# Layer 1's cross-attention in a two-layer decoder: scores on row halves, mask by a product, values stationary on column quarters

## The chip, the cores and the metric

The kernel is one program on one core of a Trainium2 chip. TensorE (PE) multiplies into PSUM; VectorE (DVE), ScalarE (ACT) and GpSimd (POOL) work on the results; SyncE (SP) issues most transfers. The metric is the device time of one execution in microseconds, the median of the runs shown.

## What is computed

Two decoder layers on x of 2 x 1024 x 256, f32. Each layer is attention, cross-attention to a context of 64 tokens, and a feed-forward part, each followed by a residual sum and a layer norm. The change concerns layer 1's cross-attention:

```python
qh = (q @ wq.T).reshape(bs, sq, N_HEADS, D_K).transpose(0, 2, 1, 3)      # 16 heads of 16
kh = (k @ wk.T).reshape(bs, sk, N_HEADS, D_K).transpose(0, 2, 1, 3)      # k = v = ctx_1024, 64 tokens
vh = (v @ wv.T).reshape(bs, sk, N_HEADS, D_K).transpose(0, 2, 1, 3)
z = jnp.einsum('bhqd,bhkd->bhqk', qh, kh) / math.sqrt(D_K)
z = jnp.where(mask[:, None, :, :], jnp.float32(-10000000000.0), z)
z = jax.nn.softmax(z, axis=-1)
z = jnp.einsum('bhqk,bhkd->bhqd', z, vh)
return z.transpose(0, 2, 1, 3).reshape(bs, sq, D_MODEL) @ wo.T
x = _layernorm(x + ...)
```

## The kernel before

The parts run one after the other: `l0_attn`, `l0_xattn`, `l0_ffn` (eight experts, 32 steps of one expert and one group of 512 rows), `l1_attn`, `l1_xattn`, `l1_ffn`. A group is 512 rows (NG = 4), a tile 128 rows (NT = 16), four tiles to a group.

`prepare` makes what layer 1 needs (transposed weights, `lxkT`, `vblk`, the mask, the quantised feed-forward weights). It is a generator: from step 4 of `l0_ffn` on, each step asks it for one piece (up to its next `yield`), and after the last step the rest is taken. Before the change it has 24 pieces, and 29 steps ask.

`l1_xattn` first spreads the keys: `kblk` (line 1644, VectorE) holds for each batch the 64 keys of each head in that head's 16 rows and zero elsewhere, so that one product of 128 rows and 512 columns makes the scores of eight heads. Then, tile by tile:

- `queries(g)`: the queries of a group, transposed (line 1661), scaled on the way out of PSUM by ScalarE and VectorE.
- `softmax(n)`: GpSimd fills a tile `lxp` with -1e10 (line 1673), two products make the 1024 scores (line 1676), VectorE copies those that the mask keeps over the fill (line 1680), takes the maximum of each head (line 1685), GpSimd subtracts it (line 1686), ScalarE takes the exponential (line 1687).
- `turn(n)`: eight transposes (line 1697) and two copies, one by ScalarE and one by VectorE.
- `mix(n)`: eight products with the turned weights stationary and `vblk` moving, 34 columns each; every head's block has a column of ones, so that the sum of the exponentials comes out beside the values (line 1712). VectorE takes the reciprocal (line 1717) and multiplies (line 1719).
- `back(n)`: two transposes of the result (line 1729). `output(n)`: the product with wo (line 1743), the residual, and at the third and fourth tile of a group the layer norm and the maximum of |x| into `xm` (line 1756), which `l1_ffn` starts from.

The last group of `l1_attn` is still open here: `ends` are its four last steps (transposes at 1394, output product at 1409 added to r = x + bias, the norm, transposes of the result at 154).

Only TensorE's order is written out by hand in this part; the order on the other engines is the scheduler's:

```python
queries(0); softmax(0); softmax(1)
for n in range(NT + 3):
    if n < 4: self.ends[n]()
    if n % 4 == 1 and n // 4 + 1 < NG: queries(n // 4 + 1)
    softmax(n + 2)
    if n < NT: turn(n)
    output(n - 3); back(n - 2); mix(n - 1)
```

PSUM: `bank()` rotates over three buffers, `wide()` (scores) over two, `acc()` is one.

Of the kernel before, what the change touches and what calls it, by code (L numbers as in the profile page):

```python
# [18 lines left out]
P = 128  # L19
B, S, D = 2, 1024, 256  # L20
T = B * S
NG = 4
# [11 lines left out]
class Decoder:  # L34
# [11 lines left out]
    def pool(self, name, bufs, **kw):  # L46

        return self.tc.tile_pool(name=name, bufs=bufs, reuse_waits="tile", **kw)
# [1459 lines left out]
    def prepare(self, tmp):  # L1508
# [8 lines left out]
        self.keep = late.tile([P, T // P, SK], U8, name="keep")  # L1517
        nc.vector.tensor_scalar(self.keep, mask, 0.0, None, ALU.is_equal)
# [3 lines left out]
        )  # L1522
        yield
        wT = {}
# [42 lines left out]
        self.vblk = late.tile([P, B, 8, 2, 17], F32, name="vblk")  # L1567
        nc.gpsimd.memset(self.vblk, 0.0)
        for k in range(2):
            rows = slice(k * SK, (k + 1) * SK)  # L1570
            nc.gpsimd.memset(self.vblk[rows, :, :, k, 16:17], 1.0)
            for b in range(B):
                nc.vector.tensor_copy(
                    self.vblk[rows, b, :, k, 0:16],
                    ps[rows, b * D : (b + 1) * D].rearrange("p (m k i) -> p m k i", k=2, i=16)[:, :, k, :],
                )
# [60 lines left out]
    def l1_xattn(self):  # L1637
# [4 lines left out]
        for b in range(B):  # L1642
            for m in range(2):
                nc.vector.tensor_tensor(
                    kblk[:, b, m],
                    self.lxkT[:, m, b * SK : (b + 1) * SK].unsqueeze(1).to_broadcast(blk),
                    self.ofhead.unsqueeze(2).to_broadcast(blk), ALU.mult,
                )
        self.xm = self.late.tile([P, 2 * NG + 1], F32, name="xm")
        with ExitStack() as s:  # L1650
            pool = lambda n, k: s.enter_context(self.pool(n, k))
            qp, pp, ptp, op = pool("lxq", 2), pool("lxp", 4), pool("lxpT", 3), pool("lxo", 3)
            qT, prob, turned, tok, tokT, res, new = {}, {}, {}, {}, {}, {}, {}
            wide = [P, H, SK]

            def queries(g):
                qT[g] = qp.tile([P, 2, GT], F32, tag="lxqT", name="lxqT")
                for m in range(2):
                    ps = self.bank()
                    for c in range(2):  # L1660
                        nc.tensor.matmul(
                            ps, lhsT=self.lxwqT[:, c, m * P : (m + 1) * P], rhs=self.xT[g][:, c, :],
                            start=c == 0, stop=c == 1,
                        )
                    self.evac(qT[g][:, m, :], ps, 0.25)

            def softmax(n):

                if n >= NT:
                    return  # L1670
                g, i = divmod(n, 4)
                p = pp.tile(wide, F32, tag="lxp", name="lxp")
                nc.gpsimd.memset(p, -1e10)
                ps = self.wide()
                for m in range(2):
                    nc.tensor.matmul(
                        ps[:, m, :], lhsT=qT[g][:, m, i * P : (i + 1) * P],
                        rhs=kblk[:, g // 2, m].rearrange("p h k -> p (h k)"), start=True, stop=True,
                    )
                nc.vector.copy_predicated(  # L1680
                    p, self.keep[:, n, :].unsqueeze(1).to_broadcast(wide),
                    ps.rearrange("p m (h k) -> p (m h) k", k=SK),
                )
                nm = self.sm.tile([P, H], F32, tag="lxnm", name="lxnm")
                nc.vector.tensor_reduce(nm, p, AX.X, ALU.max, negate=True)
                nc.gpsimd.tensor_tensor(p, p, nm.unsqueeze(2).to_broadcast(wide), ALU.add)
                nc.scalar.activation(p, p, AF.Exp)
                prob[n] = p

            def turn(n):  # L1690
                p = prob.pop(n)
                turned[n] = ptp.tile([P, 8, P], F32, tag="lxpT", name="lxpT")
                for half in range(2):
                    ps = self.bank()
                    for k in range(4):
                        m = half * 4 + k
                        nc.tensor.transpose(
                            ps[:, k * P : (k + 1) * P],
                            p[:, 2 * m : 2 * m + 2, :].rearrange("p h k -> p (h k)"), self.ident,
                        )  # L1700
                    self.evac(
                        turned[n][:, half * 4 : half * 4 + 4, :], ps.rearrange("p (k q) -> p k q", q=P),
                        by=nc.vector if half else nc.scalar,
                    )

            def mix(n):

                if not 0 <= n < NT:
                    return
                ps = self.acc()[:, 0 : H * 17].rearrange("p (h i) -> p h i", i=17)  # L1710
                for m in range(8):
                    nc.tensor.matmul(
                        ps[:, 2 * m : 2 * m + 2, :], lhsT=turned[n][:, m, :],
                        rhs=self.vblk[:, n // 8, m].rearrange("p a i -> p (a i)"), start=True, stop=True,
                    )
                rz = self.sm.tile([P, H], F32, tag="lxrz", name="lxrz")
                nc.vector.reciprocal(rz, ps[:, :, 16])
                tok[n] = op.tile([P, D], F32, tag="lxtok", name="lxtok")
                nc.vector.tensor_tensor(
                    tok[n].rearrange("p (h i) -> p h i", i=16), ps[:, :, 0:16],  # L1720
                    rz.unsqueeze(2).to_broadcast([P, H, 16]), ALU.mult,
                )

            def back(n):
                if not 0 <= n < NT:
                    return
                ps = self.bank()
                for c in range(2):
                    nc.tensor.transpose(
                        ps[:, c * P : (c + 1) * P], tok[n][:, c * P : (c + 1) * P], self.ident  # L1730
                    )
                tokT[n] = op.tile([P, 2, P], F32, tag="lxtokT", name="lxtokT")
                self.evac(tokT[n].rearrange("p c q -> p (c q)"), ps[:, 0:D], by=nc.scalar)

            def output(n):
                if not 0 <= n < NT:
                    return
                g, i = divmod(n, 4)
                if i == 0:
                    res[g] = self.rp.tile([P, 4, D], F32, tag="r", name="r")  # L1740
                ps = self.bank()[:, 0:D]
                for c in range(2):
                    nc.tensor.matmul(
                        ps, lhsT=tokT[n][:, c, :], rhs=self.lxwoT[:, c, :], start=c == 0, stop=c == 1
                    )
                nc.vector.tensor_tensor(res[g][:, i, :], ps, self.x[g][:, i, :], ALU.add)
                if i == 1:
                    new[g] = self.xp.tile([P, 4, D], F32, tag="x", name="xg")
                tiles = {2: range(3), 3: range(3, 4)}
                if g == NG - 1:  # L1750
                    tiles = {1: range(2), 2: range(2, 3), 3: range(3, 4)}
                tiles = tiles.get(i)
                if tiles:
                    self.normalise(new[g], res[g], tiles)
                    k = 2 * g + i - (1 if g == NG - 1 else 2)
                    nc.vector.tensor_reduce(
                        self.xm[:, k : k + 1], new[g][:, tiles.start : tiles.stop, :], AX.XY, ALU.max,
                        apply_absolute_value=True,
                    )
                if i == 3:  # L1760
                    self.x[g] = new[g]

            with self.tc.manual_schedule(engines={mybir.EngineType.PE}):
                queries(0)
                softmax(0)
                softmax(1)
                for n in range(NT + 3):
                    if n < 4:
                        self.ends[n]()
                    if n % 4 == 1 and n // 4 + 1 < NG:  # L1770
                        queries(n // 4 + 1)
                    softmax(n + 2)
                    if n < NT:
                        turn(n)
                    output(n - 3)
                    back(n - 2)
                    mix(n - 1)
# [4 lines left out]
    def l1_ffn(self, out):  # L1782
# [4 lines left out]
        with ExitStack() as s:  # L1787
# [57 lines left out]
            nc.scalar.activation(early, self.xm[:, 2 * NG :], AF.Silu)  # L1845
# [258 lines left out]
```

## Time and profile before

| what | value |
|---|---|
| time, median of 3 runs | 2337.06 us (2333.24 to 2337.58) |
| the profiled execution | 2335.84 us |
| its span in the profile | 2333.8 us |
| busy in the span: PE, DVE, ACT, POOL | 2255.8, 1666.6, 1105.9, 906.3 us |
| `l1_xattn`, first query product to last maximum | 2133.94 to 2251.62 us |

The profile's page gives busy time by engine, the chain of work that ended last, and groups of instructions: line, engine, operation, output from input with shapes, count, then busy microseconds and mean nanoseconds of one, then the engine's idle time just before them and what ended most of it. A table of stretches gives the busy time of each engine in a stretch, with the TensorE clock that was granted (1.00 is full). An f32 matmul shows as two instructions in the trace. L70, L74 and L76 are the lines of the helper that copies out of PSUM.

### The profile page before, as it was taken

To read this page: it belongs to the slowest core of one execution; us is meant where nothing else is said; L and a number is where in the kernel's file an instruction comes from. 1 tells how busy PE (TensorE), PEld (TensorE's weight loads), DVE (VectorE), ACT (ScalarE), POOL (GpSimd) and SP (SyncE) were. 2 spreads that over 40 slices of the span, in tenths; PEclk is the share of its full clock that TensorE was granted. 3 is DMA by queue.
4 is the path that set the end of the run, shared out by engine and by line. 5 is a ranking of instruction groups with operands and counts; after the bars stand their busy time and mean duration, and the time that the engine had idled before them with its cause. 6 is when DMAs were issued, how large, how long until landed. Compare 5 with 4: busy or idle time off the path is not lost.

```text
span 2333.8 us, 37082 instructions
## 1 busy us (share of the span) xinstructions
PE 2255.8 (97%) x13964; PEld 1561.0 (67%) x13969; DVE 1666.6 (71%) x2902; ACT 1105.9 (47%) x1730; POOL 906.3 (39%) x743
## 2 busy tenths in 40 slices
PE   8999999999999999999999999999999999999985
PEld 4555555555546788999999999999644454555752
DVE  6888898988787455555555565555789687995778
ACT  4666566566554322333333332333166454665356
POOL 4676576677565453333234243242200001002420
PEclk9999999999999999999999999999999999999988
DMA  6877677677686110100011001000302121210001
GB/s 157 178 174 173 151 176 176 142 181 180 140 197 147 41 62 1 41 28 13 19 31 37 19 31 37 14 1 1 75 14 49 22 42 25 47 27 1 1 1 37
DMA packets 103830, 168.67 MB, mean 72 GB/s; under 512 B 47602, under 2 KB 65508, under 8 KB 103652
## 3 DMA queue, kind: packets, MB, share of 16 engines
q1 hardware_dynamic: 96804, 147.94, 27.8%
q10 hardware_dynamic: 6848, 18.36, 3.2%
q8 instruction: 111, 1.82, 0.3%
q14 instruction: 67, 0.55, 0.1%
HBM read 34.10 MB, written 2.10 MB: 16 GB/s over the span
## 4 chain that ended last, share of the span: by engine, by line
PE 85%; DVE 9%; ACT 2%; issue 2%; DMA 1%; SPq 0%; POOL 0%; ACTq 0%; DVEq 0%; POOLq 0%
PE unit L1025 16%; PE acc L1073 10%; PE wide L325 9%; PE acc L410 9%; PE bank L1073 7%; PE acc L1356 5%; PE bank L280 4%; PE bank L1285 3%; DVE most L1295 3%; PE bank L428 2%; PE bank L744 2%; PE bank L304 2%; PE wide L1330 2%; PE wide L1336 2%; PE bank L1194 1%
## 5 line engine op out<-in xcount | busy, mean ns | idle before, releaser
L340 DVE TENSOR_REDUCE nm<-wide 128x1 f32<-128x1024 f32 x256 | 300.9, 1215 | 58.7 <-PE wide L325 57.6
L1342 ACT ACTIVATE w<-wide 128x1024 f32<-128x1024 f32 x256 | 248.2, 1022 | 141.1 <-PE wide L1336 131.9
L1295 DVE TENSOR_REDUCE most<-bank 128x1 f32<-128x512 f32 x476 | 295.6, 683 | 20.3 <-PE bank L1285 20.1
L325 PE MATMUL wide<-k,q 64*128 64x512 f32 x1024 | 263.2, 623 | 8.9 <-ACT p L345 6.4
L356 POOL TENSOR_SCALAR p<-p,sums 128x1024 f32<-128x1024 f32 x128 | 143.0, 1118 | 248.3 <-DVE sums L353 248.3
L410 PE MATMUL acc<-turned,v 128*64 128x256 f32 x2048 | 235.4, 383 | 0.2
L410 PEld LDWEIGHTS acc<-turned,v 128*64 128x64 f32 x2048 | 142.3, 137 | 112.1 <-issue 35.2
L1014 ACT ACTIVATE mhT<-mhT,cols 128x256 f32<-128x256 f32 (+1 forms) x256 | 143.4, 607 | 146.5 <-DVE mhT L1042 103.4
L345 ACT ACTIVATE p<-wide,nm 128x1024 f32<-128x1024 f32 x128 | 142.7, 1115 | 120.8 <-DVE nm L340 103.8
L923 POOL TENSOR_TENSOR hs<-hs,mhT 128x1024 f32<-128x1024 f32 x31 | 102.4, 3304 | 237.5 <-DVE hs L921 220.2
L1025 PE MATMUL unit<-xT,w 128*128 128x256 f32 x768 | 182.2, 379 | 0.0
L1082 DVE SCALAR_TENSOR_TENSOR r<-acc,gates,r 128x128 f32<-128x128 f32 x256 | 77.8, 345 | 138.1 <-PE acc L1073 138.1
L370 DVE STREAM_TRANSPOSE blocks<-p 128x1024 f32<-128x1024 f32 x128 | 158.1, 1235 | 23.1 <-DMA turned<-blocks 14.8
L325 PEld LDWEIGHTS wide<-k,q 64*128 64x128 f32 x1024 | 89.8, 187 | 124.5 <-issue 78.8
L370 DVE STREAM_TRANSPOSE blocks<-r 128x1024 f32<-128x1024 f32 x128 | 153.9, 1202 | 0.0
L1025 PEld LDWEIGHTS unit<-xT,w 128*128 128x128 f32 x768 | 141.1, 191 | 16.9 <-issue 0.5
L1285 PEld LDWEIGHTS bank<-kst,qst 64*128 64x128 f32 x476 | 67.2, 187 | 127.3 <-DVE most L1295 105.9
L1285 PE MATMUL bank<-kst,qst 64*128 64x512 f32 x476 | 137.5, 475 | 15.2 <-DVE most L1295 15.0
L356 POOL TENSOR_SCALAR r<-r,sums 128x1024 f32<-128x1024 f32 x128 | 143.4, 1120 | 0.0
L345 ACT ACTIVATE r<-wide,nm 128x1024 f32<-128x1024 f32 x128 | 142.0, 1110 | 0.7 <-DVE nm L340 0.5
L180 POOL TENSOR_TENSOR rstd<-ve,nhalf 128x4 f32<-128x4 f32 (+3 forms) x17 | 14.1, 832 | 325.7 <-DVE ve L178 325.4
L1356 PE MATMUL acc<-w,v 128*32 128x512 f32 x1024 | 138.5, 613 | 0.0
(349 smaller groups left out, 4492.3 us busy)
## 6 DMA issues: line engine op xcount, KB each, us to landing
turned<-blocks SPq DMA_DIRECT2D x636, 128.0 KB, 2.4
turned<-blocks ACTq DMA_DIRECT2D x132, 128.0 KB, 2.4
w<-in_L_ffn_W SPq DMA_DIRECT2D x16, 1024.0 KB, 5.7
q<-q SPq DMA_DIRECT2D x64, 128.0 KB, 2.3
k<-k SPq DMA_DIRECT2D x32, 128.0 KB, 2.3
qst<-qh SPq DMA_DIRECT2D x48, 64.0 KB
qst<-ql SPq DMA_DIRECT2D x48, 64.0 KB, 2.3
kst<-kh SPq DMA_DIRECT2D x48, 64.0 KB, 2.3
```

The source lines that it names most:

```text
L325: nc.tensor.matmul(sc[h][:, kb, :], lhsT=q[rows, qi, at : at + P], rhs=k[rows, ki, :], start=True, stop=True,)
L340: nc.vector.tensor_reduce(nm, sc, AX.XY, ALU.max, negate=True)
L345: nc.scalar.activation(p, sc.rearrange("p a c -> p (a c)"), AF.Exp, bias=nm, accum_out=sums[:, 0, h : h + 1],)
L356: nc.gpsimd.tensor_scalar(p, p, sums[:, 1, h : h + 1], 1.0, ALU.mult, ALU.mult)
L370: nc.vector.transpose(blocks[m][:, :, :, h, qt, :], p.rearrange("p (k r q) -> p r k q", r=4, q=32))
L410: nc.tensor.matmul(av[own[h], 0:256].rearrange("p (t i q) -> p i t q", t=2, i=4), lhsT=vals[u][:, kt, own[h]], rhs=p[:, h], start=kt == 0, ...
L1025: nc.tensor.matmul(v[:, m, :], lhsT=up[e][k][:, f : f + P], rhs=self.halves[g][k], start=k in (1, 2, 5) and m == 0, stop=True, skip_group_ ...
L1073: nc.tensor.matmul(ps[at][:, m * P : (m + 1) * P], lhsT=h[k][:, c, m * P : (m + 1) * P], rhs=down[e][k][:, c, :], start=k in (1, 2, 5) and ...
L1285: nc.tensor.matmul(sc[a], lhsT=stack[b, jp, "q"][rows, q0 : q0 + P], rhs=stack[b, jp, "k"][rows, kb * 512 : (kb + 1) * 512], start=True, s ...
L1295: nc.vector.tensor_reduce(most[n][:, kb, qt, h : h + 1], sc[a], AX.X, ALU.max, negate=True)
L1342: nc.scalar.activation(slot[:, k, :], ps[k].rearrange("p a q -> p (a q)"), AF.Exp, scale=0.25)
L1356: nc.tensor.matmul(mixed[n][o : o + 32, :], lhsT=vals[b][:, kt, 17 * h : 17 * h + 32], rhs=pT[:, a, :], start=kt == 0, stop=kt == 7, tile_ ...
```

## The change

`prepare` no longer keeps an inverted mask. It builds `never`, -1e30 on the diagonal of 64 keys for each of eight heads, in both row halves, and `masked`, the mask transposed so that its keys lie on rows, twice; that takes four more pieces with 16 bf16 transposes. `vblk` loses its columns of ones. `kblk` is made by GpSimd instead of VectorE.

The scores of a tile are now a product of `masked` and `never` (which puts -1e30 where the mask is set) with the score products added to it in PSUM. Each product uses 64 rows and 256 columns, and the two row halves serve different heads. ScalarE copies the result out of PSUM. The sum of the exponentials is a reduction on VectorE, and GpSimd divides the weights (`weights`) before they are turned. Both copies of the turned weights are ScalarE's. `mix` takes two tiles at once, with `vblk` stationary and the turned weights moving, each product on 32 of the 128 columns; the result comes out transposed, and `back` is gone. The layer norm is done for two tiles at a time, its scaling on ScalarE except for the last. The order of all four engines is now the order in which the functions are called, and the pools change: `lxp` 5 buffers instead of 4, `lxpT` 2 of two tiles instead of 3 of one, `lxo` 2 instead of 3.

Lines of the changed functions, with their guards left out:

```diff
-    self.keep = late.tile([P, T // P, SK], U8, name="keep")
-    nc.vector.tensor_scalar(self.keep, mask, 0.0, None, ALU.is_equal)
...
+    self.never = late.tile([P, 8, SK], BF16, name="never")
+    own = tmp.tile([P, SK], F32, name="own")
+    nc.vector.tensor_tensor(own, self.ident[:, 0:SK], self.ident[:, SK:P], ALU.add)
+    nc.vector.tensor_scalar(
+        self.never, own.unsqueeze(1).to_broadcast([P, 8, SK]), -1e30, None, ALU.mult
+    )
+    self.masked = late.tile([P, T], BF16, name="masked")
     yield
+    for n in range(0, T // P, 4):
+        both = tmp.tile([P, 4, 2, SK], BF16, tag="both", name="both")
+        nc.vector.tensor_copy(both, mask[:, n : n + 4, :].unsqueeze(2).to_broadcast([P, 4, 2, SK]))
+        ps = self.ps_t.tile([P, 1024], BF16, tag="t", name="bankb")
+        for i in range(4):
+            nc.tensor.transpose(
+                ps[:, i * P : (i + 1) * P], both[:, i].rearrange("p a k -> p (a k)"), self.identb
+            )
+        self.evac(self.masked[:, n * P : (n + 4) * P], ps[:, 0 : 4 * P])
+        yield
...
-    self.vblk = late.tile([P, B, 8, 2, 17], F32, name="vblk")
+    self.vblk = late.tile([P, B, 8, 2, 16], F32, name="vblk")
     nc.gpsimd.memset(self.vblk, 0.0)
...
-        nc.gpsimd.memset(self.vblk[rows, :, :, k, 16:17], 1.0)
...
-            nc.vector.tensor_tensor(
+            nc.gpsimd.tensor_tensor(
                 kblk[:, b, m],
...
-        qp, pp, ptp, op = pool("lxq", 2), pool("lxp", 4), pool("lxpT", 3), pool("lxo", 3)
+        qp, pp, ptp, op = pool("lxq", 2), pool("lxp", 5), pool("lxpT", 2), pool("lxo", 2)
...
-                self.evac(qT[g][:, m, :], ps, 0.25)
+                self.evac(qT[g][:, m, :], ps, 0.25, by=nc.vector if m else nc.scalar)
-        def softmax(n):
-        def back(n):
...
+        def scores(n):
...
+            g, i = divmod(n, 4)
+            ps = raw[n] = self.wide()
+            for r, a in zip(rows, range(2)):
+                nc.tensor.matmul(
+                    ps[:, a, :], lhsT=self.masked[r, n * P : (n + 1) * P],
+                    rhs=self.never[r].rearrange("p h k -> p (h k)"), start=True, stop=True,
+                    skip_group_check=True,
+                )
+            for m in range(2):
+                for r, a in zip(rows, range(2)):
+                    nc.tensor.matmul(
+                        ps[:, a, m * 256 : (m + 1) * 256], lhsT=qT[g][r, m, i * P : (i + 1) * P],
+                        rhs=kblk[r, g // 2, m, 4 * a : 4 * a + 4, :].rearrange("p h k -> p (h k)"),
+                        start=False, stop=True, skip_group_check=True,
+                    )
+        def shifted(n):
...
+            p = prob[n] = pp.tile(wide, F32, tag="lxp", name="lxp")
+            nc.scalar.copy(p, raw.pop(n).rearrange("p a (h k) -> p (a h) k", k=SK))
+            nm = self.sm.tile([P, H], F32, tag="lxnm", name="lxnm")
+            nc.vector.tensor_reduce(nm, p, AX.X, ALU.max, negate=True)
+            nc.gpsimd.tensor_tensor(p, p, nm.unsqueeze(2).to_broadcast(wide), ALU.add)
+        def exponentials(n):
...
+            p = prob[n]
+            nc.scalar.activation(p, p, AF.Exp)
+            z = self.sm.tile([P, H], F32, tag="lxz", name="lxz")
+            nc.vector.tensor_reduce(z, p, AX.X, ALU.add)
+            rz[n] = self.sm.tile([P, H], F32, tag="lxrz", name="lxrz")
+            nc.vector.reciprocal(rz[n], z)
+        def weights(n):
...
+            p = prob[n]
+            nc.gpsimd.tensor_tensor(p, p, rz.pop(n).unsqueeze(2).to_broadcast(wide), ALU.mult)
+        def turn(n):
...
+            p, (r, k) = prob.pop(n), divmod(n, 2)
+            if k == 0:
+                turned[r] = ptp.tile([P, 8, 2 * P], F32, tag="lxpT", name="lxpT")
+            for half in range(2):
+                ps = self.bank()
+                for i in range(4):
+                    j = half * 4 + i
+                    nc.tensor.transpose(
+                        ps[:, i * P : (i + 1) * P],
+                        p[:, 2 * j : 2 * j + 2, :].rearrange("p h k -> p (h k)"), self.ident,
+                    )
+                self.evac(
+                    turned[r][:, half * 4 : half * 4 + 4, k * P : (k + 1) * P],
+                    ps.rearrange("p (k q) -> p k q", q=P), by=nc.scalar,
+                )
+        def mix(r):
...
+            ps = self.acc().rearrange("p (c q) -> p c q", c=2)
+            for c in range(2):
+                for q in range(4):
+                    o = slice(32 * q, 32 * q + 32)
+                    nc.tensor.matmul(
+                        ps[o, c, :], lhsT=self.vblk[:, r // 4, 4 * c + q].rearrange("p a i -> p (a i)"),
+                        rhs=turned[r][:, 4 * (q // 2) + 2 * c + q % 2, :], start=True, stop=True,
+                        tile_position=(0, 32 * q),
+                    )
+            turned.pop(r)
+            mixed[r] = op.tile([P, 2, 2 * P], F32, tag="lxo", name="lxo")
+            self.evac(mixed[r], ps, by=nc.scalar)
+        def output(n):
...
+            (g, i), (r, k) = divmod(n, 4), divmod(n, 2)
+            if i == 0:
+                res[g] = self.rp.tile([P, 4, D], F32, tag="r", name="r")
+            ps = self.bank()[:, 0:D]
+            for c in range(2):
+                nc.tensor.matmul(
+                    ps, lhsT=mixed[r][:, c, k * P : (k + 1) * P], rhs=self.lxwoT[:, c, :],
+                    start=c == 0, stop=c == 1,
+                )
+            nc.vector.tensor_tensor(res[g][:, i, :], ps, self.x[g][:, i, :], ALU.add)
+            if k:
+                moments[r] = self.moments(res[g], range(i - 1, i + 1))
+        def normed(r):
...
+            g, i = r // 2, 2 * (r % 2)
+            if i == 0:
+                new[g] = self.xp.tile([P, 4, D], F32, tag="x", name="xg")
+            by = nc.vector if r == NT // 2 - 1 else nc.scalar
+            self.scaled(new[g], res[g], range(i, i + 2), *moments.pop(r), by)
+            nc.vector.tensor_reduce(
+                self.xm[:, r : r + 1], new[g][:, i : i + 2, :], AX.XY, ALU.max,
+                apply_absolute_value=True,
+            )
+            if i:
+                self.x[g] = new[g]
+        engines = {
+            mybir.EngineType.PE, mybir.EngineType.DVE, mybir.EngineType.Activation,
+            mybir.EngineType.Pool,
+        }
+        with self.tc.manual_schedule(engines=engines):
+            queries(0)
+            for r in range(-1, NT // 2 + 1):
+                for n in range(2 * r + 2, 2 * r + 4):
+                    scores(n)
+                mix(r - 1)
+                for k in range(2):
+                    n = 2 * r + k
+                    weights(n)
+                    shifted(n + 2)
+                    if r < 1:
+                        self.ends[n + 2]()
+                    exponentials(n + 1)
+                    turn(n)
+                    output(n - 2)
+                normed(r - 2)
+                if r % 2 == 0:
+                    queries(r // 2 + 1)
+            normed(NT // 2 - 1)
```

## The prediction

> **What bounds the kernel now.** I read the page first: one TensorE stream carries the program (PE busy 97% of the span, 85% of the chain that ended last). The rewritten stage, layer 1's cross-attention, runs from its first query product (2133.94 us) to its last maximum of |x| (2251.62): 117.7 us. The stretch view says PE works 108.9 of them, DVE 89.0, POOL 48.9, ACT 36.3. Next the chain of waits inside the stage (start, us, what):
>
> ```profile
> PE 85%; DVE 9%; ACT 2%; issue 2%; DMA 1%; SPq 0%; POOL 0%; ACTq 0%; DVEq 0%; POOLq 0%
> ...
> 2172.08 0.87 PE bank L1743 x4
> 2172.95 0.22 PE bank L1729 x2
> 2173.16 1.71 PE acc L1712 x16
> 2174.87 3.51 PE bank L1661 x8
> 2178.39 1.72 PE wide L1676 x4
> 2180.10 0.87 PE bank L1697 x8
> 2180.98 0.87 PE bank L1743 x4
> ```
>
> PE follows PE without a hole: a tile of 128 rows costs 5.46 us (2166.62 to 2172.08), two tiles 10.9, and each group's queries 3.42 more. Softmax latency is covered, because `softmax(n + 2)` puts scores two tiles ahead of their transposes and no product waits for the tile just finished. Then the groups (mean ns before the bar's second number) that price the other engines:
>
> ```profile
> L1686 POOL TENSOR_TENSOR lxp<-lxp,lxnm 128x1024 f32<-128x1024 f32 x16 | 30.4, 1901 | 32.3 <-DVE lxnm L1685 32.3
> L1685 DVE TENSOR_REDUCE lxnm<-lxp 128x16 f32<-128x1024 f32 x16 | 19.4, 1210 | 0.0
> L1342 ACT ACTIVATE w<-wide 128x1024 f32<-128x1024 f32 x256 | 248.2, 1022 | 141.1 <-PE wide L1336 131.9 <-issue 8.1 <-ACT w L1342 0.4
> L1356 PE MATMUL acc<-w,v 128*32 128x512 f32 x1024 | 138.5, 613 | 0.0
> ```
>
> Last the stretches, cut at 3.41 us because the granted clock of this trace only changes on that grid (columns: PE, PEld, DVE, ACT, POOL busy, clock, DMA):
>
> ```profile
> 1730.58:1733.99 3.41, 1.76 (x16) 0.62 (x12) 3.27 (x10) 1.94 (x2) 1.01 (x1) 1.00 0.03 7
> 1733.99:1737.41 3.42, 3.42 (x20) 1.81 (x12) 3.22 (x8) 0.88 (x1) 1.32 (x1) 0.50 0.00 0
> 1737.41:1740.82 3.41, 3.41 (x27) 2.02 (x27) 2.43 (x4) 1.64 (x3) 1.08 (x1) 1.00 0.00 0
> ...
> 2245.99:2249.40 3.41, 1.15 (x5) 0.68 (x4) 2.97 (x10) 1.66 (x2) 0.66 (x4) 1.00 0.00 0
> 2249.40:2252.81 3.41, 0.39 (x2) 0.13 (x2) 2.14 (x7) 0.20 (x1) 0.66 (x2) 0.50 0.00 0
> 2252.81:2256.23 3.42, 2.00 (x9) 1.92 (x10) 0.64 (x4) 2.22 (x3) 0.00 (x0) 0.50 0.00 0
> ```
>
> A stretch in which PE works about half the time or less (1.76, 1.15 of 3.41) is followed by one at half clock, and full clock returns after a stretch that is nearly all work (3.42). Today the stage stays at full clock until its end.
>
> **What the change does to the engines' work.** Per two tiles PE loses 7.3 us (scores 1.71, mixing 1.71, transposing back 0.22 a tile). Scores on row halves: L325 has the same form with 512 columns, 8 instructions in 1.92 us (302.78 to 304.70 in the timeline); 256 columns make 0.95, against 1.71 now. The mask product (two bf16 halves of 512 columns) has no row; between 0.21, one 512-column pass when both halves run together, and 0.43 one after the other, I take 0.25. Mixing on column quarters: L1356 does 8 instructions of 512 columns in 0.99 us (chain), so 16 of 256 cost 1.05 (0.87 to 1.1). Transposes and output stay at 0.87 and 0.86 a tile. Sum per two tiles: 2 x (0.25 + 0.95 + 0.87 + 0.86) + 1.05 = 6.9, plus 3.42 of queries every second time: 8.6 on the mean, against 12.6. ACT gets the copy out of PSUM (1.04, by L1342), exp 1.06 and both copies of the turned weights (0.585 each): 7.4 per two tiles, plus 0.59 for the mixed values, 1.1 for the norm, 0.3 for queries. DVE has two reductions of 1.21 a tile and comes to about 8.6, POOL two products of 1.9 a tile and a root: 8.3. Were the four to overlap fully, two tiles would take 8.6.
>
> **Why they will not overlap.** All four engines now run in written order. In turn r (tiles 2r, 2r+1) PE does scores(2r+2), scores(2r+3), mix(r-1), then the transposes; ACT takes mix's result, then the copy of 2r+2; POOL does weights(2r), shift(2r+2), weights(2r+1). So nothing is ahead: weights(2r+1) waits on POOL behind the shift of 2r+2, which needs that tile's maximum, its copy on ACT behind the mixed copy, which needs mix(r-1), behind both score products, which PE reaches only after the transposes and outputs of tile 2r-1, which need weights(2r-1). From one odd tile's weights to the next: transposes 0.87, output 0.86, scores and masks 2.4, mix 1.05, mixed copy 0.59, copy 1.04, maximum 1.21, shift 1.9, weights 1.9, four hand-offs 0.3 (0.05 each, 0.13 after PE, as the timeline shows around L1676, L1685 and L1686): 12.1 us. In turns with queries 3.42 and their scaling, 0.5, lie in it too: 16.0. Today's figures are 10.9 and 14.3. Around it:
> - Start to weights(1): queries 3.4, scaling and half a score 1.4, copy 1.2, maximum 1.3, two shifts 4.1, then r = x + bias (L1402, 2386 ns), which POOL now reaches behind those shifts while DVE waits for it 4.4 us with every softmax reduction queued behind, its two additions 1.4, four statistics 2.4, sum and reciprocal 1.4, weights, shift, weights 5.9: 24.9. PE waits some 7 us in it.
> - Six turns: 14.8 (the first has no output), 16.0, 16.0 and three of 12.1: 83.1. The last, without scores: 10.0.
> - Tail: transposes, copy, mix, mixed copy behind the norm of the tiles before, outputs, sums, roots, norms one after the other: 12.6.
>
> Sum 130.6, against 117.7: +12.9 at full clock. With the cheap end of every PE price 128, with the dear end 133.
>
> **The clock.** In every turn PE now stands still in one piece, after its last output until weights(odd): 12.1 less 6.9 less a hole of 1.1, about 4.1 us; in turns with queries up to 5.2. A hole that long leaves some 3.41 us stretch less than half worked, so by the rows shown each turn costs a fall to half clock, and the return needs a whole stretch of work: 3.4 to 6.8 us of PE time at half speed, 1.7 to 3.4 lost on the loop, less where the fall comes late in the hole. Seven turns and the start: 8 falls. I take 1.75 each, the low end, 14 us (0 to 20).
>
> The Trainium skill (TensorE: Matmul & The Clock Gate, "What's actually happening") has the clock fall after at least one idle window of about 3.4 us; the trace disagrees, it falls after 1.15 us of work in 3.41. By that rule a hole of 4.1 us would cover a whole window in about one turn of three, and the clock would cost an estimated 5 us.
>
> **The rest.** `prepare` puts four more jobs into the expert stage, where PE sets the pace: 16 bf16 transposes at 0.1 (L1595's loads take 99 ns) are 1.6; each job's transposes wait for DVE's `both`, as L1562 waits 1.1 us for `twice`, and the expert products queue behind; L1532, fed by a DMA, waits for nothing. I take half, 2.0: together +3.6 (1.6 to 6). DVE's copies lie in idle time (L1082 waits 138 us for PE). The jobs go from 24 to 28, and 29 steps take one; the feed-forward weights' loads on SP move with them by four steps, the period of the expert loads, so they stand behind the same kind of load and get the buffer four steps later: nothing. kblk on POOL instead of DVE: four at 0.95 to 1.27, free to start where L1644 did, 2127.1, done by 2132.2; the first score needs it at 2137.4, so nothing; uncovered it would be 5. The layer's feed-forward part starts at half clock in both.
>
> Sum: 12.9 + 14 + 3.6 = +30.5. The profiled execution took 2335.84 us (span 2333.8 and 2.0 around it), 1.2 under the median 2337.06; I add to the median: 2367.
>
> **Rivals.**
> 1. The clock holds, because a score stretch and a transposing stretch fall into each 3.41 us: +12.9 + 3.6, so 2354 (2347 to 2360). For it: a stretch with 1.72 us of work kept its clock early in the program. Against: holes of 4 to 5 us.
> 2. Faster: the loop does not bind, and turns take the busiest engine's 8.6. Then 24.9 + 7 x 8.6 + 12.6 = 97.7, with 3.6 in the experts 16 less than now: 2321. It decides from the point where a mean turn falls under (117.7 - 3.6 - 37.5) / 7 = 10.9 us; my mean is 13.3, and the cheap ends take at most 0.4 off. For it: every engine's own sum is smaller than PE's now. Against: the order of each queue.
> 3. The halves don't run together: scores 1.71 and mask 0.43 a tile, mix up to double. Each loop gains about 2.9: 7 x 2.9 more, 2387; with PE busier the clock may hold, and it ends near 2375. L325 and L1356 speak against it.
>
> **How the numbers follow.** Forecast with falling clock 0.65 (own range 2358 to 2378), clock holds 0.18, halves apart 0.07, overlap 0.08, something else about no change 0.02. The range from 2347 (cheap PE prices, no fall of the clock, 1.6 in the experts, 2 us for hand-offs counted too dear) to 2380 (dear prices 133 and 20 of clock, 6 in the experts make 2378) leaves out rival 2 and most of rival 3. This kernel's measurement can tell about 0.2%, 4.7 us, from no change: faster 0.08, same 0.02, slower 0.90.
>
> **What would show it.** After the change the stage should be near 145 us, with POOL's shift the link between DVE and the next weights, one PE hole of 4 to 5 us per two tiles ended by POOL's lxp, ACT waiting for `acc`, and stretches at clock 0.50 in the stage. POOL and DVE at over 90% busy in the stage with no such hole would show rival 2 and prove the prediction wrong; holes with clock 1.00 rival 1; 64-row score products of 1.7 us a tile rival 3.

## The result, and the profile after

The changed kernel takes 2372.18 us (median of 4 runs, 2370.33 to 2372.94), the kernel before 2337.32 in the same runs: a ratio of 1.0145, 95% interval 1.0123 to 1.0166, so 34.9 us slower. Its profiled execution took 2371.48 us, with a span of 2369.4. The span grew by 35.6 us, and it can be cut into four pieces: the rewritten stage 144.3 us in place of 117.7 (+26.6), the experts of layer 0 +5.9, layer 1's self-attention +0.6, and +2.5 that were already there at the first expert product, in code that the change does not touch. The last two are within the scatter between executions (see What stays open). The stage's length is firm: in the three runs below that leave it as it is (picks on ScalarE, casts first, and both) it takes 144.1, 144.6 and 145.0 us.

The page of the changed kernel, busy time of PE, the row of the granted clock in 40 slices, and the chain that ended last by engine:

```profile
PE 2248.8 (95%) x13916; PEld 1548.1 (65%) x13921; DVE 1653.9 (70%) x2864; ACT 1137.2 (48%) x1770; POOL 925.1 (39%) x744
...
PEclk9999999999999999999999999999999999998888
...
PE 83%; DVE 9%; ACT 2%; DMA 2%; issue 2%; POOL 1%; SPq 1%; ACTq 0%; DVEq 0%; POOLq 0%
```

PE is busy 7 us less than before (2255.8), and the kernel is slower. The slices from the stage on show 8 for the clock. The chain of waits, one turn of two tiles (start, us, what), from the weights of one odd tile to the weights of the next:

```profile
2184.61 1.91 POOL lxp L1726
2186.52 0.04 issue
2186.57 1.50 PE bank L1738 x8
2188.07 1.71 PE bank L1772 x4
2189.78 0.54 PE wide L1690 x2
2190.32 1.02 PE wide L1697 x8
2191.34 0.22 PE wide L1690 x2
2191.56 0.86 PE wide L1697 x8
2192.42 1.04 PE acc L1755 x16
2193.47 0.02 issue
2193.49 0.59 ACT lxo L74
2194.08 0.92 ACT lxp L1707
...
2195.09 1.23 DVE lxnm L1709
...
2196.48 1.36 POOL lxp L1710
2197.84 0.50 issue
2198.34 1.91 POOL lxp L1726
```

Every link of the loop that the prediction spelled out stands there in its order: weights, transposes, output, both tiles' masks and scores, the mix, its copy, the score copy, the maximum, the shift, weights. Before, PE followed PE here almost without a hole. The groups of the stage (busy, mean ns, idle time of the engine before them and what ended it) say the same by sums:

```profile
L1726 POOL TENSOR_TENSOR lxp<-lxp,lxrz 128x1024 f32<-128x1024 f32 x16 | 30.4, 1901 | 4.5 <-DVE lxrz L1720 4.5
L1738 PE MATMUL bank<-ident,lxp 128*128 128x128 f32 x128 | 25.4, 363 | 42.5 <-POOL lxp L1726 42.5
L1710 POOL TENSOR_TENSOR lxp<-lxp,lxnm 128x1024 f32<-128x1024 f32 x16 | 30.5, 1904 | 37.9 <-DVE lxnm L1709 37.9
L1709 DVE TENSOR_REDUCE lxnm<-lxp 128x16 f32<-128x1024 f32 x16 | 19.4, 1212 | 22.1 <-ACT lxp L1707 21.9 <-issue 0.2
```

PE waits 42.5 us for POOL's weights, POOL 37.9 for DVE's maximum, DVE 21.9 for ACT's copy: each engine is idle because the one before it in the loop is, and none is near full. The stretches, cut within 0.05 us of where this trace changes its clock (columns: stretch, us; then PE, PEld, DVE, ACT, POOL busy, granted clock, DMA share, GB/s):

```profile
2180.23:2183.65 3.42, 1.52 (x10) 1.06 (x8) 2.19 (x2) 3.42 (x6) 0.89 (x1) 1.00 0.00 0
2183.65:2187.06 3.41, 0.49 (x4) 0.49 (x5) 3.05 (x5) 1.67 (x2) 3.41 (x3) 1.00 0.00 0
2187.06:2190.47 3.41, 3.41 (x14) 2.48 (x14) 0.91 (x3) 1.17 (x2) 1.31 (x1) 0.51 0.00 0
2190.47:2193.89 3.42, 2.95 (x34) 1.65 (x30) 0.95 (x5) 0.40 (x1) 2.29 (x2) 0.99 0.02 5
```

The hole in which PE waits for POOL (0.49 us of work in 3.41) is followed by one stretch at half clock, and after one full stretch the clock is back. That is why, in the chain above, the transposes take 1.50 us and the outputs 1.71, where at full clock, in the kernel before, they took 0.87 each. It happens in each of the six turns from weights(3) on.

The second piece, the experts. A step here runs from one sum of L921 to the next. Who waited for the casts of the mask, in the view of their line (waiter, us, times):

```profile
L1531 DVE CAST both<-mask x4: 414/414/417, 991.3 to 1069.5; 128x512 bf16<-128x512 uint8 x4
...
  PEld L1534: 4.9, 4
  PE bankb L1534: 4.1, 4
```

The four steps with a mask job last 26.08 us each (the sums of L921 start at 973.74, 999.82, 1025.90, 1051.98, 1078.06), the step ahead of them 24.59. Four times the difference is 6.0.

### The profile page after: what moved, and what is told of

It is laid out like the page before. It is cut to its first block, busy times and chain, and to the rows that moved or that the text cites. A ratio compares the mean times of both kernels' runs of the same rounds, so it can differ in the third digit from the quotient of the medians.

```text
span 2369.4 us, 36971 instructions
## 1 busy us (share of the span) xinstructions
PE 2248.8 (95%) x13916; PEld 1548.1 (65%) x13921; DVE 1653.9 (70%) x2864; ACT 1137.2 (48%) x1770; POOL 925.1 (39%) x744
## 4 chain that ended last, share of the span: by engine, by line
PE 83%; DVE 9%; ACT 2%; DMA 2%; issue 2%; POOL 1%; SPq 1%; ACTq 0%; DVEq 0%; POOLq 0%
PE unit L1025 16%; PE acc L1073 10%; PE wide L325 9%; PE acc L410 8%; PE bank L1073 7%; PE acc L1356 5%; PE bank L280 4%; PE bank L1285 3%; DVE most L1295 3%; PE bank L428 2%; PE bank L744 2%; PE bank L304 2%; PE wide L1330 2%; PE wide L1336 2%; DMA turned<-blocks 1%
## 5 line engine op out<-in xcount | busy, mean ns | idle before, releaser
L1285 PE MATMUL bank<-kst,qst 64*128 64x512 f32 x476 | 137.7, 476 | 15.1 <-DVE most L1295 14.8
L180 POOL TENSOR_TENSOR rstd<-ve,nhalf 128x4 f32<-128x4 f32 (+1 forms) x16 | 13.8, 861 | 345.2 <-DVE ve L178 318.6
```

The costliest lines, as they stand in the source:

```text
L1285: nc.tensor.matmul(sc[a], lhsT=stack[b, jp, "q"][rows, q0 : q0 + P], rhs=stack[b, jp, "k"][rows, kb * 512 : (kb + 1) * 512], start=True, s ...
```

## The experiments

The theory: the stage is slow because its written order makes one loop through all four engines, and the holes that the loop leaves on PE halve its clock. The rival: the new operations are slow in themselves, on PE or on ACT, whatever their order. Each run differs from the changed kernel only by what its diff shows, the last by three of these diffs together; `...` marks lines that are left out.

### Scores a turn ahead

```diff
                 queries(0)
+                scores(0)
+                scores(1)
                 for r in range(-1, NT // 2 + 1):
-                    for n in range(2 * r + 2, 2 * r + 4):
-                        scores(n)
+                    if r % 2 == 0:
+                        queries(r // 2 + 1)
                     mix(r - 1)
                     for k in range(2):
                         n = 2 * r + k
                         weights(n)
                         shifted(n + 2)
+                        scores(n + 4)
...
-                    if r % 2 == 0:
-                        queries(r // 2 + 1)
```

> The changed kernel with one thing moved: the score products (and the queries that they read) are called a turn earlier, right after the copy that frees their bank pair, so that they lie on TensorE ahead of the mix. Nothing is added or left out. Theory (the loop through weights, turn, mix, scores, copy, maximum, shift sets the time): both tiles' score products, 0.86 us each in the trace of the changed kernel, leave the loop of each of 7 turns of two tiles, 7 x 1.7 = 12 us at full clock; about 2360 us, 2356 to 2366, and the stage some 132 us. Rival (the new products and the copies are slow in themselves, the order is innocent): 2372, within 3 us.

Measured: 2359.89 us (2355.67 to 2362.36), ratio to the kernel before 1.0081 (1.0062 to 1.0099), against 1.0145 for the changed kernel. The stage took 127.0 us (2148.8 to 2275.8), 17.3 less than 144.3. The seven turns, from weights(1) to weights(15), fell from 103.8 us to 84.8. The stage as a whole (its first query product to its last maximum), in the changed kernel and in this one:

```profile
2143.00:2287.30 144.30, 93.71 (x545) 62.91 (x543) 75.12 (x144) 64.95 (x93) 69.32 (x46) 0.85 0.00 1
2148.80:2275.80 127.00, 88.65 (x546) 59.51 (x544) 75.11 (x145) 64.18 (x94) 69.71 (x46) 0.90 0.00 1
```

The gain is more than the 12 expected, and the clock has a part in it: its mean rose from 0.85 to 0.90, and it falls five times in the stage where it falls nine times in the changed kernel's. The theory stands; the rival does not, since not one operation was made cheaper. That the time came out at the expected 2360 is partly luck: in the profiled execution some 6 of the 17.3 us were lost again ahead of the stage, in code that is the same (the stage starts at 2148.8 and not at 2142.9).

### The copy of the mix after the score copy

```diff
+            moved = {}
...
+                moved[r] = ps
+
+            def taken(r):
+                if not 0 <= r < NT // 2:
+                    return
                 mixed[r] = op.tile([P, 2, 2 * P], F32, tag="lxo", name="lxo")
-                self.evac(mixed[r], ps, by=nc.scalar)
+                self.evac(mixed[r], moved.pop(r), by=nc.scalar)
...
                         shifted(n + 2)
+                        if k == 0:
+                            taken(r - 1)
```

> The changed kernel with one thing moved: ScalarE's copy of the mix is called after the copy of the even tile's scores and not ahead of it; the score products stay where they are. Theory (the same loop, cut at another link): in the chain of a turn the mix, 1.04 us, and its copy, 0.59 us, stand ahead of the score copy and leave the loop, 7 x 1.6 = 11 us at most; the copy of the mix then stands before the outputs and gives part back; 2361 to 2366, a gain of 6 to 11 us. Rival (only the score products' own place on TensorE matters, as the run with scores ahead could also be read): within 2 us of the changed kernel.

Measured: 2363.82 us (2358.10 to 2371.99), ratio 1.0104 (1.0071 to 1.0136). The interval overlaps the changed kernel's, so the time alone does not settle it. In the profiled execution the stage took 137.7 us, 6.6 less, and the seven turns 96.8, 7.0 less. So the score products need not move at all for the loop to shorten: cutting it at ACT does it too. The turns fall short of the 11 us, and the trace shows two things that take from the gain. A second loop comes forward, in which the copy of the mix now holds up the exponential of the odd tile (chain of waits):

```profile
2195.44 0.59 ACT lxo L74
2196.03 0.96 ACT lxp L1718
...
2197.01 1.23 DVE lxz L1720
...
2198.34 0.26 DVE lxrz L1722
...
2198.73 1.91 POOL lxp L1728
```

And the clock got worse, 0.82 over the stage in place of 0.85: here the hole ends so late that the stretch behind it is not full either (2.64 of 3.41), and the half clock lasts for two stretches, not one:

```profile
2196.50:2199.91 3.41, 1.05 (x6) 0.60 (x4) 2.35 (x4) 3.32 (x5) 2.40 (x2) 1.00 0.00 0
2199.91:2203.33 3.42, 2.64 (x11) 2.46 (x12) 2.00 (x3) 1.17 (x2) 2.63 (x2) 0.50 0.01 2
2203.33:2206.74 3.41, 3.41 (x7) 1.68 (x6) 1.67 (x7) 0.53 (x2) 0.55 (x1) 0.50 0.00 0
2206.74:2210.15 3.41, 3.38 (x15) 1.46 (x15) 1.38 (x2) 1.16 (x3) 2.03 (x2) 1.00 0.00 0
```

### The hole filled with useless products

```diff
                 for half in range(2):
                     ps = self.bank()
+                    if half == 0 and (k or n == 0):
+                        for _ in range(3 if k else 7):
+                            nc.tensor.matmul(
+                                ps, lhsT=self.lxwqT[:, 0, 0:P], rhs=self.xT[0][:, 0, :], start=True, stop=True
+                            )
```

> The changed kernel with useless products added: three of 512 columns (some 0.65 us at full clock) on TensorE ahead of each odd tile's first transposes, seven ahead of tile 0's, into the bank that the transposes then overwrite. They are queued behind no wait that the transposes do not have too, and fill part of the hole before them. Theory (each turn has one 3.41 us window with too little TensorE work in it and pays about 1.75 us for the half clock that follows): the granted clock in the stage goes from about 0.85 to 0.95 or more and the time falls by 8 to 12 us, to 2360 to 2364. Rival (the half clock lies beside other engines' work and costs nothing): no gain, and up to 5 us lost where a product comes late and the transposes stand behind it; 2372 to 2377.

Measured: 2367.94 us (2365.87 to 2372.64), ratio 1.0120 (1.0101 to 1.0138). The useless products were dearer than expected: three of them take 2.84 us at full clock and not 0.65, and still fit into the holes of the changed kernel's turns, 3.5 to 5.0 us long from weights(3) on. The clock of the stage went from 0.85 to 0.96, and in the seven turns it did not fall until their last 0.3 us (the stretches around one hole, columns as above):

```profile
2184.76:2188.17 3.41, 2.59 (x12) 1.28 (x11) 3.04 (x5) 1.46 (x3) 3.41 (x3) 1.00 0.00 0
2188.17:2191.58 3.41, 3.41 (x29) 2.40 (x26) 1.64 (x7) 1.02 (x2) 1.43 (x2) 1.00 0.02 5
2191.58:2195.00 3.42, 2.23 (x28) 1.55 (x27) 0.68 (x1) 2.29 (x3) 2.21 (x2) 1.00 0.00 0
```

The seven turns took 94.0 us against 103.8: between the weights of odd tiles lie 16.0, 12.1, 15.9, 12.1, 15.9, 12.1 and 10.0 us. The last six are the cleanest measurement of the loop at full clock, 78.1 against 87.4, so the clock costs 9.4 in them. The first turn is not: useless products stand in its chain (3.51 us), partly at half clock. The stage as a whole gained only 6.4 (137.9), because the end gave 3.3 back: the products ahead of tile 15 stand behind tile 14's outputs and not in a hole (they took 3.75 us in the chain and its transposes 0.87 more; without them the transposes took 1.83, at half clock), and the last outputs then fell into a half clock (3.69 against 2.01). The expectation of 8 to 12 for the time was too high for that reason; for the turns it holds.

### The mask's casts ahead of their transposes

```diff
+        first = tmp.tile([P, 6 * D], BF16, tag="fwq", name="fwq").rearrange("p (n a k) -> p n a k", a=2, k=SK)
+        rest = tmp.tile([P, 4, 2, SK], BF16, name="both")
         for n in range(0, T // P, 4):
-            both = tmp.tile([P, 4, 2, SK], BF16, tag="both", name="both")
+            both = first[:, n : n + 4] if n < 12 else rest
             nc.vector.tensor_copy(both, mask[:, n : n + 4, :].unsqueeze(2).to_broadcast([P, 4, 2, SK]))
+        yield
+        for n in range(0, T // P, 4):
+            both = first[:, n : n + 4] if n < 12 else rest
...
             self.evac(self.masked[:, n * P : (n + 4) * P], ps[:, 0 : 4 * P])
-            yield
+            if n != 8:
+                yield
```

> The changed kernel with the four casts of the mask (0.41 us each on VectorE) made together one step of the experts ahead of their first transposes; the 16 transposes and four evictions stay, the last two groups of them in one step, so that the number of pieces is the same. Theory (TensorE stands still for each cast, 1.04 us in each of the four steps by its idle time): four waits go, -4.2 us, about 2368; 2366.5 to 2369.5. Rival (the price of a mask step, 1.49 us, is the transposes, their evictions and the shifted order of the later pieces): -1 to 0.

Measured: 2373.30 us (2367.44 to 2375.00), ratio 1.0135 (1.0115 to 1.0155). By the time this looks like the rival. By the trace of the profiled execution (2374.18 us) it does not: the experts, from the first to the last sum of L921, took 777.8 us (870.1 to 1647.9) against 782.7 in the changed kernel, 4.9 less, and nothing waits for the casts any more. The gain was lost again in layer 1's self-attention, which took 8.4 us more than in the changed kernel's. Part of that lies at its start, some 20 us after the experts, where VectorE casts `pick` while GpSimd sets memory. The timeline of the changed kernel and then of this one (start, us, engine, operation; two casts, two memsets and one more):

```profile
1674.17 0.70 DVE L1221 CAST pick<-w 128x128 fp32r<-128x128 f32 x2
...
1674.19 1.14 POOL L1225 MEMSET cz<- 128x512 f32 x2
1675.28 2.02 POOL L1236 MEMSET v<- 128x2304 f32 x1
```

```profile
1668.28 3.12 DVE L1221 CAST pick<-w 128x128 fp32r<-128x128 f32 x2
...
1668.30 0.99 POOL L1225 MEMSET cz<- 128x512 f32 x2
1669.23 2.02 POOL L1236 MEMSET v<- 128x2304 f32 x1
...
1672.58 0.50 PE L1285 MATMUL wide<-kst,qst 64*128 64x512 f32 x2 [2.28 <-DVE most L1290]
```

In both the cast begins 0.02 us before the memset. In one it is over in 0.70 us; in the other it ends at 1671.40, 0.15 after the last memset, and VectorE's next operation, for which PE waits 2.28 us, starts late. That hole is followed by a stretch at clock 0.54, in which eight products of L1242 take 3.61 us and not 1.99. Together that is 3.9 us; the other 4.5 is within the scatter that the next runs show.

### The picks on ScalarE, without and with the casts first

```diff
-                nc.vector.tensor_copy(pick[k], f)
+                nc.scalar.copy(pick[k], f)
```

That line alone:

> The changed kernel with one line of layer 1's self-attention moved from VectorE to ScalarE: the two casts of pick, which lie at the same moment as GpSimd's memsets. In the trace of the changed kernel they take 0.60 us each, in that of casts first 3.02 us, until the memset beside them ends. It is the comparison for the next run. Theory and rival agree here: within 1.5 us of the changed kernel, a ratio of 1.0140 to 1.0150 to the kernel before.

Measured: 2373.66 us (2371.20 to 2377.67), ratio 1.0145 (1.0121 to 1.0169), as the changed kernel. With the casts first as well:

> Casts first, as in the run before, and the two casts of pick on ScalarE. Theory (the casts of the mask cost 4.9 us in the experts, and the run of casts first lost that again where VectorE's casts of pick stood behind GpSimd's memsets: 2.28 us of idle TensorE and the half clock after it): 4 to 6 us less than with the picks alone, ratio about 1.012. Rival (what the experts gain is lost later whatever the picks do): within 1.5 us of the picks alone, ratio about 1.0142.

Measured: 2369.47 us (2367.19 to 2374.43), ratio 1.0128 (1.0103 to 1.0153). The medians are 4.2 us apart, as the theory has it, but the runs of the two overlap, and so do the intervals. What is firm is the piece that was changed: 777.8 us for the experts again, in place of 782.7, and the wait of 2.28 us is not there. Why the times scatter more than that gain can be seen in all ten traces: from the last sum of the experts to the first query product of the rewritten stage they show between 487.6 and 494.0 us, for code that is nearly the same (497.4 with the stalled casts). That scatter was not traced further.

### All of the stage in another order

Each step of a tile becomes a function of its own, and a turn is a list. No operation is added or left out.

```diff
+            based(3)
             self.ends = [lambda f=f: f(3) for f in (turned, output, normed, onward)]
...
+                for r in range(-4, NT // 2 + 5):
+                    for f, at in (
+                        (highest, 2 * r + 2),
+                        (exponentials, 2 * r + 1),
+                        (mix, r - 1),
+                        (weights, 2 * r),
+                        (taken, r - 1),
+                        (root, r - 2),
+                        (summed, 2 * r + 1),
+                        (copied, 2 * r + 3),
+                        (shifted, 2 * r + 2),
+                        (normed, r - 2),
+                        (asked, r + 2),
+                        (ending, 2 * r + 2),
+                        (highest, 2 * r + 3),
+                        (turn, 2 * r),
+                        (output, 2 * r - 2),
+                        (scores, 2 * r + 4),
+                        (weights, 2 * r + 1),
+                        (exponentials, 2 * r + 2),
+                        (summed, 2 * r + 2),
+                        (output, 2 * r - 1),
+                        (shifted, 2 * r + 3),
+                        (ending, 2 * r + 3),
+                        (copied, 2 * r + 4),
+                        (turn, 2 * r + 1),
+                        (scores, 2 * r + 5),
+                        (measured, r - 1),
+                    ):
+                        if 0 <= at < last[f]:
+                            f(at)
```

(`copied`, `highest` and `shifted` are the copy, the maximum and the subtraction of the old `shifted`; `taken` is the copy of the mix, `asked` the queries, `ending` one of `self.ends`, `summed` the sum of the exponentials and its reciprocal, `measured` and `root` the statistics and POOL's root, `based` makes r = x + bias, called before the stage.)

> The changed kernel with all its operations, none added or left out, issued in another order: scores a turn ahead, ScalarE's copy of a score pair away from the copy of the mix, the exponential, the sums and the weights of a tile each a tile ahead of its transposes, and the residual with its bias made before the stage. Theory (the change is slow only through the loop that the order makes; each engine's own work in the stage is 67 to 76 us): the stage takes 95 to 110 us in place of 144, the kernel about 2330, 2322 to 2345, and so no slower than the kernel before. Rival (the changed operations are themselves what is slow): the order is worth no more than the scores ahead, 2355 to 2366.

Measured: 2330.54 us (6 runs, 2326.33 to 2334.30), ratio to the kernel before 0.9954 (0.9939 to 0.9968). The stage took 101.4 us (columns as above):

```profile
2149.20:2250.60 101.40, 83.25 (x546) 53.06 (x544) 79.45 (x144) 64.11 (x93) 67.21 (x45) 0.98 0.00 1
```

The changed kernel's stage, shown above, is 144.3 us: its PE is busy 10 us longer at the lower clock, its POOL 2 us longer because r = x + bias still lies in it, its DVE 4 us less. The operations are the same. The seven turns took 68.9 us, 9.85 each, and POOL's weights are hardly waited for now, 3.6 us in place of 42.5 (PE's transposes, idle before them and what ended it):

```profile
L1750 PE MATMUL bank<-ident,lxp 128*128 128x128 f32 x128 | 18.9, 287 | 6.3 <-POOL lxp L1738 3.6 <-ACT lxqT L76 2.3
```

In the chain from 2185 to 2230 us, the middle of this stage, DVE's two reductions are the largest lines now (15.2% and 15.0%). So the changed operations are not what is slow; the order of their issue is.

### Order, casts and picks together

> The other order of the stage, casts first and picks on ScalarE together: all operations of the changed kernel, none added or left out. Theory (the gains lie in different stages and add up): some 42 us less than the changed kernel by the order and 5 by the casts, 2325 to 2329, ratio about 0.993 to the kernel before. Rival (the casts' gain is lost again): as the order alone, ratio 0.9954.

Measured: 2323.60 us (2319.51 to 2324.31), ratio to the kernel before 0.9930 (0.9905 to 0.9956), 50 us under the changed kernel with the picks alone. The stage took 101.6 us and the experts 777.8 again. It beats both kernels; the expected 2325 to 2329 was 1 us too high. Against the order alone (0.9954) the intervals overlap: that the casts' gain is kept is firm in the experts, not in the time.

## Why the prediction was right

**The loop.** It was worked out link by link to 12.1 us a turn, 16.0 with queries and 10.0 for the last. The filled hole, which takes the clock out of it, measured 12.1, 15.9 and 10.0. The first turn was put at 14.8 and took 16.4; no run shows it at full clock. PE's holes, put at 4.1 us and up to 5.2 with queries, took 3.5 to 5.0 from weights(3) on. The prices of the links were close: mask pair 0.22 against 0.25, scores 0.86 against 0.95, mix 1.04 against 1.05, score copy 0.92 in the chain against 1.04, maximum 1.23 against 1.21, shift and weights 1.90 as taken. That products on 64 rows and on 32 columns of the array run side by side, which rival 3 doubted, is shown by the first three: one after the other it had put the scores at 1.71 a tile and the mix at up to double.

**The clock.** Eight falls were forecast, one at the start and one for each turn. The changed kernel has them: at the start, in the six turns from weights(3) on, and one ahead of the tail; a ninth comes 1.3 us before the stage ends, where the kernel before has one as well. Each was put at 1.75 us; in the six turns one cost 1.4 to 1.65 (17.5 against 15.9, 13.7 against 12.1). What the fall at the start cost is not measured. The rival that the clock holds (2354) fails on the rows. The page of the Trainium skill that the prediction weighed (TensorE: Matmul & The Clock Gate, "What's actually happening") asks for a whole idle window of about 3.4 us before a fall. In the changed kernel the eight stretches ahead of those falls held 0.21, 0.49, 0.41, 0.00, 0.00, 0.00, 0.10 and 1.41 us of PE work, so only three were wholly idle, and the last of the eight came 2.0 us into a hole. The measurement decides for "half worked or less".

**Start and end.** The start was put at 24.9 us up to the end of weights(1) and took 27.1 (2143.03 to 2170.13): the sum had left out VectorE's norm of the residual (L228, 3.67 us in the chain), which stands between a maximum and the next sum. The tail was put at 12.6 and took 13.4. Start, turns and tail make 27.1 + 103.8 + 13.4 = 144.3, where "near 145" stood. That it is so near is partly luck. Of the 14 us for the falls the six turns used 9.4; the other 4.6 were made up by start, first turn and tail, which took 4.6 more than their terms at full clock (2.2, 1.6 and 0.8), in the start by the norm that was left out and not by the clock.

**The experts: the step that was mis-sized.** They cost 5.9 us and not 3.6. The transposes cost no more than was taken: with the casts ahead of them 5.9 - 4.9 = 1.0 us is left, under the 1.6 for sixteen loads. The wait was wrong: the prediction saw one line of `prepare` that waits 1.1 us for VectorE and one, fed by a DMA, that does not, and took half. Each of the four waited 1.04 on PE, and the two runs with the casts ahead put the price at 4.9 in all. A cast that is issued right before the product that reads it is a wait, not half a wait.

**Faster by overlap: rival 2.** It was worked out at 2321 us, from turns of the busiest engine's 8.6, and the prediction set the point at which it decides at a mean turn of 10.9. The changed kernel's turns take 14.8. In another order the same operations take 9.85 (9.87 in the last run) and the kernel 2330.5, with casts and picks 2323.6. So the rival's mechanism was real, and what the prediction held against it, the order of each queue, was most of what stood in its way; what keeps 9.85 from 8.6 was not tried. One sum behind the 8.6 has a slip: ScalarE's terms make 6.5 us for two tiles and not 7.4, and with 7.4 and what is added to it ScalarE, not PE, would have been the busiest. The 8.6 holds by the terms.

**What stays open.** The 2.5 us before the experts and the 0.6 of the self-attention need not be an effect of the change: over the ten profiled executions, whose code is the same up to there, the first expert product starts between 833.9 and 840.4 us (837.4 in the changed kernel, 834.9 before), and the self-attention scatters by 6. What makes that scatter is open.

## What to carry to other kernels

When work is taken from the engine that sets the pace and given to others, count the loop from one use of a queue to the next and not only the engines' sums: here every sum in the stage lay below 95 us and the stage rose to 144. Before such a change is given up, reorder the queues so that each step of a tile is issued a tile before it is read; the same operations then took 101. And a hole on TensorE costs more than its own length where it leaves a stretch of the clock's grid half empty.

## What the runs showed of the hardware

The clock. In the profiles of six of these kernels (before, changed, scores ahead, filled hole, reordered, mix copy later), in and around the stage, the granted clock changes only on a grid of 3.413 us, whose place differs from run to run. All 26 stretches at full clock with 1.4 us of PE work or less were followed by half clock. Of four with 1.47 to 1.56 us two were; those with more kept it, but for one with 2.04 us after a stretch of 1.74. (Outside the stage, the prediction's rows have one with 1.76 us that was followed by half clock.) From half clock, no stretch with 2.65 us or less brought full clock back; all of those with 3.2 us or more did, and between 2.7 and 3.1 it went both ways. PE's ends are modelled in these records, so the bounds are good to some tenths.

VectorE beside GpSimd. The two casts of 128x128 on VectorE lie beside memsets of GpSimd in every trace where they are on VectorE. They took 0.31 us each in the kernel before, where a memset of 0.5 us had begun 0.26 earlier; 0.60 in the changed kernel and four runs, beginning 0.02 us ahead of that memset; and 3.02 in one execution, until the memsets were over, with the same 0.02 us between the starts. On ScalarE, in another place of the queue, a cast took 0.30 in three executions. What decides between 0.60 and 3.02 was not found.
